# Moving the product of the next unit by one piece, in a pipelined convolution and wavelet kernel

## The chip, the cores and the metric

The kernel runs on one core of a Trainium2 chip. The metric is the device time of one execution in microseconds (us), lower is better. Engines are named as the profile names them: PE does the matrix products (PEld is its weight loads), DVE, ACT and POOL do the elementwise work, and SP issues the transfers.

## What is computed

The reference applies four layers to an image batch `x` of shape (4, 64, 256, 256): batch, channel, row, column.

```python
# layers 0, 2, 3: a long convolution in rows and columns with filters made by a small network
k = einsum('ijk,imk->ijmk', hx, hy)[0]            # separable: an x filter and a y filter per channel
y = irfft2(rfft2(x, 512) * rfft2(k, 512) / 512)[..., :256, :256]
x = y + x * bias[:, None, None]

# layer 1: mixing of channels in the Haar wavelet domain
f1 = haar2d(x)
for i in range(2):
    f3 = f1 * v[i]                                # v[i]: one value per row and column
    f4 = einsum('bchw,oc->bohw', f3, conv_w[i])   # 64 channels to 64 channels
    acc += sign(f4) * relu(abs(f4) - tau[i])      # soft threshold
x = haar2d(acc, inverse=True) + x
```

Since `v[i]` does not depend on the channel, the kernel multiplies by the channel matrix first and by `v[i]` afterwards.

## The kernel before

**Tiling.** The four images are handled as two groups of two images (`GROUPS = 2`, `NB = 2`). For the convolutions and the wavelets a round `t` holds two channels of the two images of a group, so there are 32 rounds in a group (`ROUNDS`) and 64 in all. A filter is a Toeplitz matrix. The function `toeplitz` multiplies a block of 64 rows by it with 16 small matrix products; the function `haar` applies a wavelet matrix with 4.

**Phases.** Phase A does layer 0 and the forward wavelet, round by round. Phase B does the channel mixing of layer 1, once for each group. Phase C does the inverse wavelet and layers 2 and 3, round by round. The phases are written as lists of Python functions, called pieces. The helper `beside(main, side, lead, tail)` calls the pieces of a main list in order and spreads the pieces of a side list evenly between them. The kernel sets the order of instructions by hand (`manual_schedule`): each engine executes its instructions in the order in which the pieces issue them, and semaphores make it wait where data or a buffer is not ready.

**The stretch that matters here.** The mixing of the second group, `phase_b(1)`, is the side list beside the first rounds of phase C (line 1048). The main list has 525 pieces. The side list has 404: the start with its 13 pieces, three pieces for each of 130 values of `u`, and one more. They are spread over the last 514 main pieces, which is 0.786 side pieces for each main piece: after a main piece comes one side piece or none. A step `s` of the mixing is one of 64 sets of coefficients; each step has two units, `u = 2s` and `u = 2s + 1`, one for each of the two mixings `i`. For the second group the odd units are "raw" from step 2 on (`raw`, line 573): their product is only copied out, and its threshold is done later, in phase C.

**A unit.** The product of unit `u` is `mix(u)`: four matrix products with 512 columns into the PSUM tile `f4`. This tile has one buffer:

```python
un[u]["f4"] = bps.tile([P, NB, W], F32, tag="f4", name=f"f4_{grp}_{u}", bufs=1)
```

`multiply(u)` on DVE empties it: line 670 multiplies it by `v` into `x` (even units), or line 667 copies it to `raw` (odd units). The next product can be written only when that has been done. The further steps of an even unit are `sign` (ACT, line 676), `magnitude` (ACT, line 685), `less` (DVE, line 690), `threshold` (DVE, line 695) and `add` (POOL, lines 710, 713 and 714), which accumulates into `gt`; `store` sends it to DRAM. `exchange` (ACT, line 701) swaps the two halves of an image for `add`, and `store_raw` (line 727) sends the raw product out.

The three pieces `j = 0, 1, 2` of `phase_b(1)` issue, for a value of `u`:

| piece | PE | DVE | ACT | POOL | SP |
|---|---|---|---|---|---|
| j = 0 | | `multiply(u)`, `less(u-1)` | | `add(u-2)` | `store` |
| j = 1 | `mix(u+1)` | `threshold(u-1)` | `sign(u)` | | `store_raw`, `load_v` |
| j = 2 | | | `magnitude(u)`, `exchange` | | `load_f` |

**What runs beside it.** A round of phase C has 18 pieces: 16 Toeplitz pieces (rows and columns of the layers 2 and 3; tiles `c1r`, `c1c`, `c2r`, `c2c`) and two wavelet pieces (tile `c0ps`). The results lie in PSUM banks. There are six banks for them in this stretch (`rings`, line 1044), which are used in turn, two at a time. ACT empties the row results (`ch`, line 907) and most of the wavelet results (`z`, line 895), and DVE the column results (`cy` and `o`, line 926). These copies wait in a list that is issued at the start of the following piece (`flush`). POOL does the inverse wavelet along the free axis (line 429, tiles `i` and `ci`), one operation in each main piece.

Of the kernel before, what the change touches and what calls it, by code (L numbers as in the profile page):

```python
# [67 lines left out]
GROUPS = 2  # L68
# [32 lines left out]
def conv_haar_kernel(  # L101
# [194 lines left out]
    def half(r):  # L296
        return slice(r * ROW, (r + 1) * ROW)
# [270 lines left out]
    def phase_b(grp):  # L568

        units = 2 * STEPS  # L570
        mixers = []

        def raw(u):
            return grp == GROUPS - 1 and u % 2 == 1 and FULL <= u // 2 < STEPS
# [11 lines left out]
        def load_f(s):  # L586
            if s >= STEPS:
                return
            d = st[s]
            d["f"] = bp.tile([P, NB, W], F32, tag="ft", name=f"ft_{grp}_{s}", bufs=4)  # L590
            rows, f = step_of(coef[grp], s, d["f"])
            nc.sync.dma_start(f, rows)

        def load_v(s):
            if s >= STEPS:
                return
            d = st[s]
            d["v"], d["tau"] = [], []

            def fetch(first, count, tag):  # L600
                t = bp.tile([P, 2, count, W], F32, tag=tag, name=f"{tag}_{grp}_{first}_{s}", bufs=3)
                at = slice(first * W, (first + count) * W)
                nc.sync.dma_start(t[:, 0].rearrange("p i w -> p (i w)"), v[s, :, at])
                of = thresholds[s].rearrange("r c w -> (r c) w")[:, at].unsqueeze(1).to_broadcast([2 * SHARED, C // SHARED, count * W])
                nc.sync.dma_start(t[:, 1].rearrange("p i w -> p (i w)"), of)
                d["v"] += [t[:, 0, i] for i in range(count)]
                d["tau"] += [t[:, 1, i] for i in range(count)]

            fetch(0, 2 if grp < GROUPS - 1 else 1, "v")
            if grp == GROUPS - 1 and not raw(2 * s + 1):  # L610
                fetch(1, 1, "raw")
# [20 lines left out]
        def part():  # L632

            a, b, c, d, t, u = four("g", half(0), slice(0, NB))
            op = nc.gpsimd.tensor_tensor
            op(t, a, b, ALU.add)
            op(b, a, b, ALU.subtract)
            nc.gpsimd.tensor_scalar(u, c, math.sqrt(2.0), None, ALU.mult)
            op(a, t, u, ALU.add)
            nc.gpsimd.tensor_scalar(d, d, math.sqrt(2.0), None, ALU.mult)  # L640
            op(c, b, d, ALU.add)
            op(d, b, d, ALU.subtract)
            op(b, t, u, ALU.subtract)

        def mix(u):
            s, i = divmod(u, 2)
            un[u]["f4"] = bps.tile([P, NB, W], F32, tag="f4", name=f"f4_{grp}_{u}", bufs=1)
            for b in range(NB):
                for r in range(2):
                    q = r ^ b  # L650
                    nc.tensor.matmul(  # L651
                        un[u]["f4"][half(q), b, :],
                        mixers[0][half(r), bass.ts(i, C)],
                        st[s]["f"][half(r), b],
                        start=True,
                        stop=True,
                        tile_position=(r * ROW, q * ROW),
                    )
# [5 lines left out]
        def multiply(u):  # L664
            if raw(u):
                t = st[u // 2]["raw"] = bp.tile([P, NB, W], F32, tag="raw", name=f"raw_{grp}_{u}", bufs=3)
                nc.vector.tensor_copy(t, un[u]["f4"])
                return
            un[u]["x"] = bp.tile([P, NB, W], F32, tag="x", name=f"x_{grp}_{u}", bufs=2)
            nc.vector.tensor_tensor(un[u]["x"], un[u]["f4"], both(u, "v"), ALU.mult)  # L670

        def sign(u):
            if raw(u):
                return
            un[u]["m"] = bp.tile([P, NB, W], F32, tag="m", name=f"m_{grp}_{u}", bufs=3)
            nc.scalar.activation(un[u]["m"], un[u]["x"], AF.Sign)  # L676

        def magnitude(u):
            if raw(u):
                return  # L680
            if grp == GROUPS - 1:
                un[u]["a"] = un[u]["x"]
            else:
                un[u]["a"] = bps.tile([P, NB, W], F32, tag="a", name=f"a_{grp}_{u}", bufs=1)
            nc.scalar.activation(un[u]["a"], un[u]["x"], AF.Abs)

        def less(u):
            if raw(u):
                return
            nc.vector.tensor_tensor(un[u]["a"], un[u]["a"], both(u, "tau"), ALU.subtract)  # L690

        def threshold(u):
            if raw(u):
                return
            nc.vector.scalar_tensor_tensor(un[u]["m"], un[u]["a"], 0.0, un[u]["m"], ALU.max, ALU.mult)  # L695

        def exchange(s):

            st[s]["other"] = bp.tile([P, W], F32, tag="other", name=f"other_{grp}_{s}", bufs=2)
            for q in range(2):  # L700
                nc.scalar.copy(st[s]["other"][half(q)], st[s]["f"][half(1 - q), 1])

        def add(u):
            s, i = divmod(u, 2)
            if raw(u):
                un[u].clear()
                return
            m = un[u]["m"]
            if i:
                nc.gpsimd.tensor_tensor(st[s]["g"], st[s]["g"], m, ALU.add)  # L710
            else:
                g = st[s]["g"] = bp.tile([P, NB, W], F32, tag="gt", name=f"gt_{grp}_{s}", bufs=3)
                nc.gpsimd.tensor_tensor(g[:, 0], m[:, 0], st[s]["f"][:, 0], ALU.add)  # L713
                nc.gpsimd.tensor_tensor(g[:, 1], m[:, 1], st[s]["other"], ALU.add)
            un[u].clear()

        def store(s):
            to, g = step_of(mixed[grp], s, st[s]["g"])
            nc.sync.dma_start(to, g)
            st[s].clear()  # L720

        def store_raw(s):
            if s < FULL:
                t = st[s]["raw"] = bp.tile([P, NB, W], F32, tag="raw", name=f"none_{grp}_{s}", bufs=3)
                nc.gpsimd.memset(t, 0.0)
            to, g = step_of(unshrunk, s, st[s]["raw"])
            nc.sync.dma_start(to, g)

        def piece(u, j):

            s, i = divmod(u, 2)
            if j == 0:
                if u < units:
                    multiply(u)
                if 0 < u <= units and grp == GROUPS - 1:
                    less(u - 1)
                if 1 < u <= units + 1:
                    add(u - 2)
                if i == 0 and s == 3:
                    part()  # L740
                    store(0)
                    store(1)
                if i == 0 and s > 3 and not raw(2 * s - 3):
                    store(s - 2)
                if i and raw(2 * s - 1):
                    store(s - 1)
            elif j == 1:
                if 0 < u <= units and grp < GROUPS - 1:
                    less(u - 1)
                if u + 1 < units:  # L750
                    mix(u + 1)
                if u < units:
                    sign(u)
                if i and s < STEPS and grp == GROUPS - 1:
                    store_raw(s)
                if 0 < u <= units:
                    threshold(u - 1)
                if i == 0 and s > 0:

                    load_v(s + 2)  # L760
                    if grp < GROUPS - 1:
                        load_f(s + 3)
            else:
                if i and s > 0 and grp == GROUPS - 1:
                    load_f(s + 3)
                if u < units:
                    magnitude(u)
                if i == 0 and s < STEPS:
                    exchange(s)
# [10 lines left out]
        for u in range(units + 2):  # L780
            for j in range(3):
                pieces.append(lambda u=u, j=j: piece(u, j))
        pieces.append(lambda: piece(units + 2, 0))
        return pieces

# [390 lines left out]
```

## Time and profile before

| what | value |
|---|---|
| time, median of 3 runs (lowest to highest) | 2503.36 us (2502.98 to 2511.66) |
| the profiled execution: its time and its span | 2502.12 us, 2500.3 us |
| busy PE, PEld | 91%, 74% of the span |
| busy POOL, DVE, ACT | 83%, 71%, 56% of the span |

The span runs from the first to the last instruction; the time has 1.8 us around it. "Busy" is the share of time with at least one instruction of the engine in execution. Matrix products overlap each other, so a PE that is busy is not necessarily at its full rate.

The second group's mixing (from the first product `f` to the last) lies between about 1082 and 1784 us of the span; the stretch from 1160 to 1790 us is its even part.

### The profile page before, as it was taken

To read this page: it belongs to the slowest core of one execution; us is meant where nothing else is said; L and a number is where in the kernel's file an instruction comes from. 1 tells how busy PE (TensorE), PEld (TensorE's weight loads), DVE (VectorE), ACT (ScalarE), POOL (GpSimd) and SP (SyncE) were. 2 spreads that over 40 slices of the span, in tenths; PEclk is the share of its full clock that TensorE was granted. 3 is DMA by queue.
4 is the path that set the end of the run, shared out by engine and by line. 5 is a ranking of instruction groups with operands and counts; after the bars stand their busy time and mean duration, and the time that the engine had idled before them with its cause. 6 is when DMAs were issued, how large, how long until landed. Compare 5 with 4: busy or idle time off the path is not lost.

```text
span 2500.3 us, 119287 instructions
## 1 busy us (share of the span) xinstructions
PE 2266.2 (91%) x53298; PEld 1839.1 (74%) x53298; DVE 1775.7 (71%) x1943; ACT 1392.4 (56%) x2318; POOL 2079.4 (83%) x2428
## 2 busy tenths in 40 slices
PE   7999999777777777887999999999899999999999
PEld 5777897444444444665777777777799999989998
DVE  4533335799999999765777777777577777777763
ACT  1233233577777777254666666666565655555652
POOL 2889887999999999778777877777879999999990
PEclk9999999899999999888999999999999999999999
DMA  6788888699999999557888998999866666666653
GB/s 187 249 285 293 296 304 303 253 367 357 360 339 363 342 357 330 201 203 271 314 320 315 322 327 314 323 317 326 273 208 214 208 222 217 211 209 216 216 165 111
DMA packets 222968, 688.03 MB, mean 275 GB/s; under 512 B 31470, under 2 KB 32815, under 8 KB 218232
## 3 DMA queue, kind: packets, MB, share of 16 engines
q1 hardware_dynamic: 222456, 680.40, 77.8%
q8 instruction: 419, 6.86, 1.1%
q14 instruction: 93, 0.76, 0.1%
HBM read 428.16 MB, written 252.12 MB: 272 GB/s over the span
## 4 chain that ended last, share of the span: by engine, by line
PE 45%; DVE 5%; DMA 2%; issue 2%; POOL 2%; ACT 1%; SPq 1%; DVEq 0%; ACTq 0%; POOLq 0%
PE c2c L340 10%; PE c2r L340 10%; PE c1r L340 9%; PE c1c L340 8%; PE c0ps L352 4%; PE f L651 4%; DVE m L695 1%; DVE cy L926 1%; DVE x L670 1%; DVE x L690 1%; DMA g<-mixed 1%; POOL i L429 0%; DMA rows<-in_v_rows 0%; ACT ch L907 0%; DVE o L926 0%
## 5 line engine op out<-in xcount | busy, mean ns | idle before, releaser
L429 POOL TENSOR_TENSOR i<-i,g 128x16 f32<-128x16 f32 x744 | 439.6, 612 | 27.2
L651 PE MATMUL f<-ft,mix 64*64 64x512 f32 x2048 | 290.9, 614 | 142.5 <-DVE x L670 123.0
L340 PEld LDWEIGHTS a2ps<-toep,ay 64*64 64x64 f32 x8192 | 296.0, 136 | 119.8 <-DVE f L521 48.1
L340 PE MATMUL a2ps<-toep,ay 64*64 64x128 f32 (+3 forms) x8192 | 335.4, 303 | 19.7 <-DVE f L521 15.6
L340 PEld LDWEIGHTS c2c<-toep,ch 64*64 64x64 f32 x8192 | 299.0, 135 | 58.8 <-issue 25.8
L340 PEld LDWEIGHTS c1c<-toep,ch 64*64 64x64 f32 x8192 | 299.5, 133 | 45.0 <-issue 20.3
L340 PEld LDWEIGHTS a1ps<-toep,x 64*64 64x64 f32 x8192 | 280.0, 135 | 65.1 <-issue 33.5
L429 POOL TENSOR_TENSOR ci<-i,g 128x1024 f32<-128x1024 f32 x124 | 317.5, 2581 | 4.5
L340 PE MATMUL a1ps<-toep,x 64*64 64x128 f32 (+3 forms) x8192 | 315.1, 300 | 6.1 <-DMA toep<-filt 2.4
L340 PEld LDWEIGHTS c1r<-toep,z 64*64 64x64 f32 x8192 | 294.0, 135 | 35.1 <-issue 18.0
L340 PE MATMUL c1r<-toep,z 64*64 64x192 f32 (+3 forms) x8192 | 313.5, 299 | 5.5 <-issue 3.7
L340 PE MATMUL c2c<-toep,ch 64*64 64x128 f32 (+3 forms) x8192 | 311.0, 299 | 7.7 <-ACT ch L907 7.2
L340 PEld LDWEIGHTS c2r<-toep,cy 64*64 64x64 f32 x8192 | 290.9, 134 | 29.0 <-issue 15.6
L340 PE MATMUL c2r<-toep,cy 64*64 64x192 f32 (+3 forms) x8192 | 309.9, 298 | 1.7 <-issue 1.5
L340 PE MATMUL c1c<-toep,ch 64*64 64x192 f32 (+3 forms) x8192 | 306.8, 296 | 1.7 <-ACT ch L907 1.2
L713 POOL TENSOR_TENSOR gt<-m,ft 128x512 f32<-128x512 f32 x128 | 163.6, 1278 | 159.6 <-DVE m L695 159.2
L907 ACT COPY ch<-c2r 128x512 f32<-128x512 f32 x256 | 137.3, 590 | 281.5 <-PE c2r L340 280.8
L488 ACT COPY ay<-a1ps 128x512 f32<-128x512 f32 x256 | 137.4, 589 | 273.5 <-PE a1ps L340 272.9
L676 ACT ACTIVATE m<-x 128x1024 f32<-128x1024 f32 x194 | 206.0, 1062 | 149.3 <-DVE x L670 101.0
L670 DVE TENSOR_TENSOR x<-f,v 128x1024 f32<-128x1024 f32 x192 | 233.3, 1215 | 18.5 <-PE f L651 17.9
L508 DVE SCALAR_TENSOR_TENSOR x<-x,bias_sb,a2ps 128x512 f32<-128x512 f32 x256 | 179.4, 742 | 91.4 <-POOL f L390 44.5
L926 DVE SCALAR_TENSOR_TENSOR o<-cy,bias_sb,c2c 128x512 f32<-128x512 f32 x256 | 176.8, 742 | 89.3 <-PE c2c L340 87.7
(86 smaller groups left out, 3921.5 us busy)
## 6 DMA issues: line engine op xcount, KB each, us to landing
toep<-filt SPq DMA_DIRECT2D x768, 112.0 KB
ft<-coef SPq DMA_DIRECT2D x128, 512.0 KB
mixed<-gt SPq DMA_DIRECT2D x128, 512.0 KB
g<-mixed SPq DMA_DIRECT2D x256, 256.0 KB
x<-in_x SPq DMA_DIRECT2D x128, 256.0 KB
coef<-f SPq DMA_DIRECT2D x128, 256.0 KB
x<-in_x SPq DMA_DIRECT2D x32, 1024.0 KB
v<-in_v SPq DMA_DIRECT2D x64, 512.0 KB
```

Of the source, the lines that this page charges most:

```text
L340: nc.tensor.matmul(ps[r][half(c), j % 2, k * ROW :], data[half(r), c, k, bass.ts(j, ROW)], t(r, c)[:, : N - k * ROW], start=k == 0, stop=k ...
L352: nc.tensor.matmul(ps[r][half(c)].rearrange("p h k -> p (h k)"), matrix[half(r)], pairs(r, c).rearrange("p h k -> p (h k)"), start=True, s ...
L429: engine.tensor_tensor(to, s, d, op)
L488: later(lambda y=y, ps=ps: nc.scalar.copy(y, ps))
L508: nc.vector.scalar_tensor_tensor(to, old, bias_sb[:, c : c + 1], ps, ALU.mult, ALU.add)
L651: nc.tensor.matmul(un[u]["f4"][half(q), b, :], mixers[0][half(r), bass.ts(i, C)], st[s]["f"][half(r), b], start=True, stop=True, tile_posi ...
L670: nc.vector.tensor_tensor(un[u]["x"], un[u]["f4"], both(u, "v"), ALU.mult)
L676: nc.scalar.activation(un[u]["m"], un[u]["x"], AF.Sign)
L690: nc.vector.tensor_tensor(un[u]["a"], un[u]["a"], both(u, "tau"), ALU.subtract)
L713: nc.gpsimd.tensor_tensor(g[:, 0], m[:, 0], st[s]["f"][:, 0], ALU.add)
L907: later(lambda y=y, ps=ps: nc.scalar.copy(y, ps))
L926: nc.vector.scalar_tensor_tensor(to, of, bias_sb[:, at : at + 1], ps, ALU.mult, ALU.add)
```

## The change

The call of `mix(u + 1)` is taken out of piece `j = 1` for the second group and put at the head of piece `j = 2`. For the first group it stays where it was.

```diff
             elif j == 1:
                 if 0 < u <= units and grp < GROUPS - 1:
                     less(u - 1)
-                if u + 1 < units:
+                if u + 1 < units and grp < GROUPS - 1:
                     mix(u + 1)
                 if u < units:
                     sign(u)
...
             else:
+                if u + 1 < units and grp == GROUPS - 1:
+                    mix(u + 1)
                 if i and s > 0 and grp == GROUPS - 1:
                     load_f(s + 3)
                 if u < units:
```

## The prediction

> **What bounds the kernel now.** I read the page first. POOL and PE are both above 80% over the whole span, so the page alone doesn't name a bound for the stretch that the change touches. I then asked for the busy time in two windows, both 630 us long: the even part of the second group's mixing, and the last stretch, where phase C runs with no mixing beside it.
>
> ```profile
> core 0: us, PE busy (x) PEld busy (x) DVE busy (x) ACT busy (x) POOL busy (x), PEclk, DMA share, GB/s
> 1160.00:1790.00 630.00, 597.88 (x14172) 484.51 (x14168) 459.60 (x437) 408.68 (x711) 473.83 (x520) 0.99 0.90 318
> 1850.00:2480.00 630.00, 629.54 (x17306) 594.82 (x17302) 444.36 (x504) 351.03 (x658) 557.65 (x558) 1.00 0.62 203
> ```
>
> PE is the fullest engine in both. With the mixing beside it, its weight loads are busy 77% of the time against 94% without. So PE has holes in the stretch, while DVE (73%), POOL (75%) and ACT (65%) have more. How much is lost: in the timeline two Toeplitz pieces take 2.18 us from start to start where nothing interrupts them, so one takes 1.09 us; a product `f` takes 0.86 us, and so does a wavelet piece. The stretch from 1160 us to the last product, 626.8 us, holds 200 pairs of Toeplitz pieces, 117 products and 50 wavelet pieces: 200 x 2.18 + 167 x 0.86 = 579 us. PE is therefore bound by its own work but for about 48 us.
>
> Where the 48 us are is told by the view of the tile `f` in this window, and by the list of waits.
>
> ```profile
> L651 PE MATMUL f<-ft,mix x936: 587/589/1057, 1162.2 to 1783.2; 64*64 64x512 f32 x188
> L670 DVE TENSOR_TENSOR x<-f,v x59: 1209/1217/1226, 1160.5 to 1781.4; 128x1024 f32<-128x1024 f32 x59
> L667 DVE COPY raw<-f x59: 1209/1223/1226, 1163.3 to 1783.8; 128x1024 f32<-128x1024 f32 x59
> its engine sat idle before it (us, times) until:
>   PE f L651: 48.9, 34
>   DVE x L670: 31.1, 28
> ```
>
> ```profile
> DVE o L926 <- PE c2c L340: 56.6, 29, 3.7
> DVE raw L667 <- PE f L651: 38.1, 26, 3.3
> DVE cy L926 <- PE c1c L340: 34.9, 17, 4.8
> DVE x L690 <- ACT x L685: 23.4, 22, 3.0
> PE f L651 <- DVE x L670: 21.2, 21, 2.8
> ```
>
> The row "until DVE x L670" is PE and its weight loads waiting, before a product, for DVE to empty the one buffer of `f4` (28 times). "Until PE f L651" is DVE waiting for the product. Read at the weight loads, product by product, 33 products start within 0.2 us of the end of the operation that emptied the tile, and the idle time before them sums to 32.0 us: two thirds of the 48. The longest are 2.86, 2.60, 2.17, 2.08, 1.88 and 1.84 us; about half are 0.5 to 0.65 us. One of them in the timeline (start, duration):
>
> ```profile
> 1449.18 2.71 DVE L926 SCALAR_TENSOR_TENSOR cy<-z,bias_sb,c1c 128x512 f32<-128x512 f32 x4
> 1451.81 1.21 DVE L670 TENSOR_TENSOR x<-f,v 128x1024 f32<-128x1024 f32 x1
> 1454.32 1.22 DVE L667 COPY raw<-f 128x1024 f32<-128x1024 f32 x1 [1.29 <-PE f L651]
> ...
> 1453.17 1.09 PE L651 MATMUL f<-ft,mix 64*64 64x512 f32 x8 [1.33 <-DVE x L670]
> 1454.05 1.73 PE L340 MATMUL c1r<-toep,z 64*64 64x256 f32 x40
> ```
>
> DVE is late with four residual operations, empties `f4` by 1453.02, and PE stands until then with a Toeplitz piece behind the product that needs nothing from DVE. Then DVE stands 1.29 us for the product. Each waits for the other in turn.
>
> **What the Trainium skill says.** "Perfetto Trace Analysis", section "Identifying the Most-Contended Engine", says that busy matmul time is a bad measure and the share of the weight loads a better one; the trace agrees (95% against 77% in this stretch). The same page, section "Optimization Strategy", says that the same gap repeating on the engine that should be full can mean that PSUM or SBUF lacks a buffer; `f4` with one buffer is this case. "SBUF — State Buffer", section "Who interferes with whom", says that a DVE operation with two SBUF inputs and a POOL operation that reads SBUF exclude each other. The trace agrees: `less` and `threshold` take 1541 and 1690 ns on average here, up to 3.2 us beside a `ci` of POOL, and 1228 and 1225 ns in the first group, where one input is in PSUM. That is why DVE's lateness varies.
>
> **The change, part by part.** Nothing is added or removed. In the built programs the order on DVE, ACT, POOL and SP is the same in both; only the products move on PE, each past the main pieces that lie between two side pieces. At 0.786 side pieces to a main piece this is one or two. Counted over units 10 to 127: 87 products move past one piece (0.85 or 1.07 us of PE's work), 31 past two (1.92 or 2.13); the mean is 1.32 us. Some DVE readers of `f4` and five loads of `ft` name PE among their waits in addition; the loads' waits are for products long past.
>
> Gain: `f4` is emptied at the same place of DVE's order, and PE has 0.85 to 2.13 us of other work ahead of the product. Each of the 33 waits becomes its old length less the moved work, or nothing. Summed one by one, 32.0 us become 4.9 us: the waits of about 0.6 us all go, and only some of the nine over 1.1 us leave a rest. Gain 27.1 us. At the start, from 1060 to 1160 us, products wait only 1.5 us for DVE, and PE's large wait there is 10.0 us for POOL's `ci`, which hangs on a long run of POOL; I cost that at 0.
>
> Loss one: `multiply` now follows its product by one side piece, not two. Behind it in DVE's order stand the residuals, `less`, `threshold` and the next `multiply`; ACT's `sign` and POOL's `add` wait for these, and behind `sign` stand the copies that free PSUM banks. With today's times held, a product moved by its amount, less PE's own saved wait, comes after the moment at which DVE reached it in 49 of 118 cases, by 40.5 us in all. This is idle time of DVE, not of PE. It is hidden if DVE has room: a step (two units) takes 626.8 / 58.5 = 10.7 us, DVE is busy 459.6 / 59 = 7.8 us of it, and waits 91.5 / 59 = 1.55 us for `c1c` and `c2c`, which takes up a delay of 40.5 / 59 = 0.69 us. Where it is not taken up, DVE is late at the next product and a wait of PE comes back: I put this at 3 us, with 0 and 27 us (the whole gain) as ends.
>
> Loss two: banks and POOL. Against today's reuse of a pair of banks, the copies have 1.4 to 3.0 us to spare in nine cases of ten, with a minimum of 0.25 us (`c1c`) and 0.45 us (`c2r`). A few will now be late by some tenths: 2 us, from 0 to 8. `ci` of POOL ends 1.6 to 8 us before its first product but for one case of 0.15 us; POOL waits 148.1 us for `threshold` and moves with DVE: 2 us, from 0 to 6. The queue of SP stands behind `store_raw` up to 1 us longer; the loads behind it are for two steps (21 us) or a round ahead: 0. After the stretch PE waits about 8 us, while ACT waits for the transfer of `rows`; the place in the order is the same: 0.
>
> Sum on the profiled execution: its time 2502.1 (span 2500.3 and 1.8 around it) - 27.1 + 3 + 2 + 2 = 2482.0 us. The median before is 1.2 us above that execution: 2483 us.
>
> **The rivals.** (1) The waits re-form. If DVE hangs on the product at each odd unit, its whole order shifts by as much as the product does, and `multiply` is late by the same amount at the next one: the deadline and the work move together. For it: DVE's 48.9 us of waits for the product, at least half of them in the same chain as PE's waits. Against it: the many waits of 0.6 us follow a residual, which is tied to PE and not to the last product. It leaves a gain of 0 to 12 us, say 2497 us. (2) Slower: DVE's chain becomes the bound. The place is odd `multiply`: from even `multiply` to the odd product now lie two side pieces, 2.55 main pieces or 2.7 us, and 0.96 us for the product with its signals; DVE's own 1.22 us lies inside, so DVE can be idle up to 2.4 us a step. With 7.8 us busy and 0.4 us for ACT this gives 10.6 us, even with today's step; it decides where DVE's waits for residuals do not shrink by what the product's wait grows. At 0.3 us a step more than today that is 59 x 0.3 = 18 us: 2521 us. Against it: PE ends the column pieces earlier as its own waits go. (3) No change, because the waits are the profile's artefact and the holes are of another kind (17 us of the 48 have no named releaser): 2503 us. Against it: start of the product and end of `multiply` agree to 0.15 us in 33 cases.
>
> **How the numbers follow.** Gain of 13 to 30 us: 0.65. Rival 1: 0.18. Rival 2: 0.12. Rival 3: 0.05. The forecast's own range is 2473 to 2490 us. The range for 8 in 10 reaches up through rival 1 and into rival 2: 2472 to 2512. A measurement of this kernel tells about 0.5% (12.5 us) from no change: faster 0.67, same 0.20, slower 0.13.
>
> **What would show it.** Right: the waits of `f` for DVE fall from 31 us to under 10 in the same stretch; the mixing ends some 20 us earlier; the last stretch has the same length; DVE's wait for the product stays or grows to 50 to 90 us. Wrong: PE's waits for `f` stay at 20 us or more (rival 1); PE waits for `ch`, `cy` or `o` in the stretch, or `c0ps` for `ci`, by more than 10 us; DVE's waits for `f` grow and those for `c1c` and `c2c` do not shrink (rival 2).

## The result

The changed kernel takes 2488.38 us (median of 4 runs, 2485.05 to 2488.89) against 2505.49 us before (4 runs), a ratio of 0.9932 with a 95% interval from 0.9912 to 0.9952. That is 17.1 us less; 20.4 us less had been forecast, with 2483 us. In a later set of runs the same kernel took 2485.01 us against 2503.35 us before, a ratio of 0.9917 (0.9901 to 0.9933), which is 18.3 us less. The profiled execution takes 2485.05 us, with a span of 2483.2 us (before: 2502.12 and 2500.3).

The busy time in windows, for the even part of the mixing (which now ends 13 us earlier, so the window is shorter) and for the last stretch:

```profile
core 0: us, PE busy (x) PEld busy (x) DVE busy (x) ACT busy (x) POOL busy (x), PEclk, DMA share, GB/s
1160.00:1770.00 610.00, 591.82 (x14038) 505.47 (x14030) 458.53 (x432) 405.05 (x706) 472.28 (x511) 1.00 0.92 327
1850.00:2480.00 630.00, 628.65 (x17328) 593.24 (x17320) 439.73 (x505) 343.33 (x644) 543.08 (x541) 1.00 0.61 200
```

PE's weight loads are busy 83% of the stretch, against 77% before. The last stretch is as it was (94%). The share is not a measure of pace: a kernel of the experiments below (the product two pieces later) shows 83% too, with just as many loads between 1160 and 1770 us as the kernel before has at 77% (13688 in both); it is the time with at least one load in execution, and loads overlap. The pace is therefore read from a part with fixed contents, from the start of the eleventh product to the start of the last, seen at the weight loads: 625.7 us before and 610.1 us after. PE's own work in that part (1.09 us for each of 397 Toeplitz pieces, 0.86 us for each of 117 products and 50 wavelet pieces) is 576 us in both kernels: 49 us of PE's time were lost before, and 34 us are now. The prediction, which counted 200 pairs of Toeplitz pieces, had 48 us.

From the view of the tile `f`, changed kernel, in the mixing from 1160 to 1775 us (the idle time of an engine before the operations on this tile, and how often):

```profile
its engine sat idle before it (us, times) until:
  PE f L651: 90.4, 55
  DVE x L670: 9.5, 11
```

PE's idle time before a product until DVE has emptied the tile falls from 31.1 us (28 times) to 9.5 us (11 times). DVE's idle time until the product is there rises from 48.9 to 90.4 us. Read at the weight loads, product by product, 33 waits of 32.0 us have become 10 of 6.1 us, all before the products of odd units.

The list of waits of the changed kernel in the same window, for DVE (total, times, longest):

```profile
DVE raw L667 <- PE f L651: 70.6, 37, 5.1
DVE o L928 <- PE c2c L340: 27.4, 20, 3.7
DVE cy L928 <- PE c1c L340: 22.0, 15, 2.8
DVE x L670 <- PE f L651: 19.8, 18, 2.6
```

DVE's waits for the product have grown by 41.5 us (from 48.9 to 90.4), and its waits for the column results have shrunk by 42.1 us (from 56.6 + 34.9 to 27.4 + 22.0). DVE has not more idle time than before, but waits at another place. And the list for the weight loads of the changed kernel from 1160 to 1770 us ("issue" is a wait with no named releaser):

```profile
PEld c1c L340 <- issue: 13.5, 37, 2.1
...
PEld f L651 <- DVE x L670: 6.1, 8, 1.7
PEld c1c L340 <- ACT ch L909: 4.1, 5, 2.3
PEld c2c L340 <- ACT ch L909: 3.6, 10, 0.8
```

The waits for the copies `ch` in the same window before:

```profile
PEld c1c L340 <- ACT ch L907: 2.8, 4, 2.1
...
PEld c2c L340 <- ACT ch L907: 0.3, 1, 0.3
```

Two kinds of waits have taken some of the gain. Weight loads wait for ACT's copies `ch` for 4.1 + 3.6 = 7.7 us (before: 2.8 + 0.3 = 3.1 us). And idle times of over 0.3 us before weight loads of Toeplitz pieces, with no named releaser, sum to 16.4 us in 17 holes (before: 8.5 us in 11). The expectations below counted these holes a little differently, as 15.0 us in 16 and 7.7 us in 10.

A smaller term goes the other way, and no theory below is about it. The clock that the trace shows as granted to PE (`PEclk` in the views: 0.99 before, 1.00 now) falls to half for 3.4 us twice in this part of the kernel before, never in the changed one and once in its repeat (see the end of this document). If half the work is done at half the clock, an estimate of 3.4 us was lost to it before, and of 0 and 1.7 us after.

### The profile page after: what moved, and what is told of

Its sections match the earlier page's. It is cut to its first block, busy times and chain, and to the rows that moved or that the text cites. A ratio compares the mean times of both kernels' runs of the same rounds, so it can differ in the third digit from the quotient of the medians.

```text
span 2483.2 us, 119306 instructions
## 1 busy us (share of the span) xinstructions
PE 2261.3 (91%) x53298; PEld 1863.9 (75%) x53298; DVE 1775.6 (72%) x1943; ACT 1392.2 (56%) x2318; POOL 2080.2 (84%) x2428
## 3 DMA queue, kind: packets, MB, share of 16 engines
q8 instruction: 419, 6.86, 1.1%
## 4 chain that ended last, share of the span: by engine, by line
PE 47%; DMA 2%; DVE 2%; issue 1%; POOL 1%; ACT 1%; SPq 0%; DVEq 0%; ACTq 0%; POOLq 0%
PE c2c L340 10%; PE c2r L340 10%; PE c1c L340 10%; PE c1r L340 9%; PE c0ps L352 4%; PE f L651 4%; DMA g<-mixed 1%; DMA toep<-filt 1%; DVE cy L928 0%; POOL i L429 0%; DVE x L670 0%; DMA unshrunk<-raw 0%; DVE x L690 0%; ACT ch L909 0%; DMA out<-o 0%
## 5 line engine op out<-in xcount | busy, mean ns | idle before, releaser
L651 PE MATMUL f<-ft,mix 64*64 64x512 f32 x2048 | 302.8, 614 | 117.6 <-DVE x L670 104.0
L340 PEld LDWEIGHTS c1c<-toep,ch 64*64 64x64 f32 x8192 | 311.8, 133 | 43.8 <-issue 14.0
L340 PEld LDWEIGHTS c2c<-toep,ch 64*64 64x64 f32 x8192 | 304.8, 134 | 51.1 <-issue 12.8
L340 PE MATMUL c1c<-toep,ch 64*64 64x128 f32 (+3 forms) x8192 | 317.2, 297 | 7.9 <-issue 4.6
L340 PE MATMUL a1ps<-toep,x 64*64 64x256 f32 (+3 forms) x8192 | 314.0, 299 | 6.7 <-issue 3.8
L340 PEld LDWEIGHTS c2r<-toep,cy 64*64 64x64 f32 x8192 | 298.5, 134 | 27.2 <-issue 12.5
L340 PE MATMUL c2r<-toep,cy 64*64 64x128 f32 (+3 forms) x8192 | 316.3, 298 | 2.9 <-issue 2.6
L909 ACT COPY ch<-c1r 128x512 f32<-128x512 f32 x256 | 137.5, 594 | 169.2 <-PE c1r L340 168.8
```

The costliest lines, as they stand in the source:

```text
L340: nc.tensor.matmul(ps[r][half(c), j % 2, k * ROW :], data[half(r), c, k, bass.ts(j, ROW)], t(r, c)[:, : N - k * ROW], start=k == 0, stop=k ...
L651: nc.tensor.matmul(un[u]["f4"][half(q), b, :], mixers[0][half(r), bass.ts(i, C)], st[s]["f"][half(r), b], start=True, stop=True, tile_posi ...
L909: later(lambda y=y, ps=ps: nc.scalar.copy(y, ps))
```

## The experiments

Theory A is that of the prediction: PE stood before a product until DVE had emptied the one buffer, and other work of PE now fills that time. The theories named B to E in the expectations are its rivals, or are about the two kinds of waits above.

### Odd products alone, even products alone

In the first kernel only the products of odd units move, in the second only those of even units:

```diff
-                if u + 1 < units:
+                if u + 1 < units and (grp < GROUPS - 1 or i):          # second kernel: or not i
                     mix(u + 1)
...
             else:
+                if u + 1 < units and grp == GROUPS - 1 and not i:      # second kernel: and i
+                    mix(u + 1)
```

> Only the products of the odd units are issued one piece later; the even ones stay where they were. Theory A (the time went because PE no longer stands before a product until DVE has emptied the one buffer): 31 us of PE's 32 us of waits stood before odd products. Moving these alone leaves about 11 us when the waits are shortened one by one, so the kernel should gain 12 to 18 us against before, nearly all of the change's 17; DVE's waits for the odd product (raw) rise from 38 us to about 65, those for the even product stay near 11. Rival B (DVE's chain shifts with the product, and waits come back at the next product, which is now the even one and not moved): PE's waits for DVE stay above 20 us and the gain is under 8 us.

> Only the products of the even units are issued one piece later. Theory A: few of PE's waits stand before even products, so they stay at about 26 us and the gain is 0 to 6 us. Rival B, and any theory in which the gain comes from having the product later in general: about half of the change's gain, 8 us or more. If the even move costs ACT and DVE more than it brings, the time is up to 5 us above before.

Odd alone: 2490.24 us, ratio 0.9948 (0.9935 to 0.9961), 13.1 us less than before. Even alone: 2501.34 us, ratio 0.9985 (0.9971 to 0.9998), 2.0 us less. The waits read at the weight loads:

| kernel | waits before odd products | before even products | eleventh to last product |
|---|---|---|---|
| before | 26.1 us (23) | 5.9 us (10) | 625.7 us |
| odd later | 9.5 us (10) | 3.1 us (13) | 615.3 us |
| even later | 23.0 us (25) | 0 | 624.6 us |
| both later (the change) | 6.1 us (10) | 0 | 610.1 us |

The gain is where the waits were, as theory A says, and the two parts together (15.1 us) come near to the whole. Rival B falls: when the odd products move, the waits before the unmoved even ones do not grow, they fall from 5.9 to 3.1 us. The expectation had put 31 of the 32 us before odd products; it was 26.1, read at the weight loads. With the even products alone the waits are 9 us shorter and the time only 2 us: in that profile the holes without a name are longer (13.6 us) and so, by the estimate above, is the loss at half the clock (8.5 us, in five falls).

### The product one piece earlier

```diff
             if j == 0:
                 if u < units:
                     multiply(u)
+                if u + 1 < units and grp == GROUPS - 1:
+                    mix(u + 1)
...
-                if u + 1 < units:
+                if u + 1 < units and grp < GROUPS - 1:
                     mix(u + 1)
```

> The product of the next unit is issued one piece earlier than before, right behind the operation that empties its buffer. Theory A: PE has 1.33 us less work, on average, ahead of each product, and shortens nothing: PE's waits for DVE rise from 32 us to as much as 95 us in the window of the mixing, so the kernel is slower than before by 35 to 63 us. Rival C (PE's holes at the product are not waits for the buffer, or DVE sets the pace of the stretch either way): the time stays within 10 us of before.

2563.41 us, ratio 1.0251 (1.0226 to 1.0277): 60.1 us slower. The waits before products are 82.7 us (52.2 odd, 30.5 even), 50.7 us more, and the part from the eleventh to the last product takes 685.9 us, 60.2 us more. The clock is at half nine times in this part, an estimated 15.4 us of PE's work against 3.4 us before, which covers the difference. The view of the tile `f` of this kernel, from 1160 to 1842 us:

```profile
its engine sat idle before it (us, times) until:
  issue: 100.3, 79
  DVE x L670: 49.5, 32
  PE f L651: 34.2, 23
```

Here most of PE's waiting goes by "issue"; the comparison of each product's start with the end of the operation that emptied the tile shows what it is. Rival C (DVE sets the pace either way) falls. DVE waits 15 us less for the product here than in the kernel before, and the kernel is 60 us slower.

### The product two pieces later

```diff
             if j == 0:
+                if 0 < u < units and grp == GROUPS - 1:
+                    mix(u)
                 if u < units:
                     multiply(u)
...
-                if u + 1 < units:
+                if u + 1 < units and grp < GROUPS - 1:
                     mix(u + 1)
```

> The product of a unit is issued in the same piece as the operation that empties it, one piece later than in the changed kernel. Theory A: PE's waits for the buffer are gone (under 2 us), but that is only some 5 us less than in the changed kernel; DVE's waits for the product rise to 150 us or more. If DVE has room for it, the time is 0 to 5 us below the changed kernel. If DVE's chain (7.8 us of work in a step of about 10.4 us, and now over 2 us of waits for products) becomes the bound, PE stands for ch, cy, o or ci, and the time is 5 to 40 us above the changed kernel; this I hold likelier.

2502.42 us, ratio 0.9996 (0.9983 to 1.0008): all of the gain is lost again. PE's waits for DVE are gone (0.3 us). The tile `f` and the waits of the weight loads, in this kernel:

```profile
  PE f L651: 149.4, 89
...
  DVE x L670: 0.3, 1
```

```profile
PEld c2c L340 <- ACT ch L909: 13.4, 23, 1.9
...
PEld c1c L340 <- ACT ch L909: 7.8, 13, 3.4
```

DVE waits 149.4 us for products, and PE waits 13.4 + 7.8 = 21.2 us for `ch`. The part from the eleventh to the last product takes 624.3 us, 14.2 us more than in the changed kernel. The waits for `ch` grow by 13.5 us and those before products shrink by 6; so about half of the 14 us has a named cause here, and the rest stays open. So the place of the product has a best value between two costs: early, PE waits for DVE; late, DVE's `multiply` is late, and with it ACT.

### What makes ch late

Five kernels ask why ACT is late. Its order in the third piece of an even unit is `magnitude` and the two copies of `exchange`, with `sign` in the piece before. First only the odd product goes one piece further, since no operation of ACT waits for it:

```diff
             if j == 0:
+                if i and u < units and grp == GROUPS - 1:
+                    mix(u)
...
-                if u + 1 < units and grp == GROUPS - 1:
+                if i and u + 1 < units and grp == GROUPS - 1:
                     mix(u + 1)
```

> Even products as in the changed kernel, odd ones one piece later still, in the piece of their own copy. The odd product feeds only the copy to raw, so no operation of ACT waits for it. PE's waits for DVE (6.1 us, all before odd products in the changed kernel) fall to under 1 us, DVE's wait for odd products rises from 71 to about 105 us. If PE's rest of 6 us is a plain gain: 3 to 6 us below the changed kernel. If DVE's lateness reaches PE through the even products and the residuals: equal to the changed kernel or up to 8 us above it.

2497.55 us, ratio 0.9975 (0.9962 to 0.9988), 12.5 us above the changed kernel in the same set of runs (2485.01 us). PE's waits before products fall to 2.6 us, but PE waits 18.8 us for `ch`. The reading that fits: the odd copy on DVE is late, the even `multiply` behind it is late with it (ACT waits 93.2 us for it, 76.2 in the changed kernel), and so ACT is late. The remaining 6 us of PE's waits were not to be had this way.

Next, `sign` is moved to the third piece, in the changed kernel and in the kernel with the product two pieces later:

```diff
-                if u < units:
+                if u < units and grp < GROUPS - 1:
                     sign(u)
...
+                if u < units and grp == GROUPS - 1:
+                    sign(u)
                 if u < units:
                     magnitude(u)
```

> The changed kernel with sign issued in the third piece of a unit too, just ahead of magnitude, so that ACT's copies of the second piece don't stand behind an operation that waits for multiply. If ACT's waiting for multiply (76 us) is what makes ch late for PE (7.7 us of PE's weight loads waiting for ch), the wait for multiply falls by half or more, that for ch to under 3 us, and the time by 2 to 5 us. If ch is late for another reason, both stay and the time is that of the changed kernel; it may rise by some us where less then waits longer for magnitude (6 us now).

> The product two pieces later than before, and sign in the third piece. With the product two pieces later PE had no waits for DVE, but its loads waited 21 us for ch, behind ACT's 125 us of waiting for multiply. If that blocking is what took the gain back, PE's waits for ch fall to under 8 us and the time by 8 to 14 us, to about 2490. If DVE's own chain is the bound, PE's waits for ch stay above 15 us or turn into waits for cy, o or ci, and the time stays at about 2502.

With the change: 2487.16 us, ratio 0.9928 (0.9913 to 0.9943). With the product two pieces later: 2499.39 us, ratio 0.9979 (0.9966 to 0.9993). ACT's wait for `multiply` nearly halves in both (76.2 to 40.3 us, and 125.7 to 65.9 us), but PE's wait for `ch` stays: 9.2 us, and 20.6 us. That ACT stands idle behind `sign` is therefore not the whole cause. The timeline of ACT in the changed kernel shows another. The first fence is ACT (start, duration), the second is PE's weight loads in the same microseconds:

```profile
1595.66 1.06 ACT L676 ACTIVATE m<-x 128x1024 f32<-128x1024 f32 x1 [3.93 <-DVE x L670]
1596.75 1.06 ACT L685 ACTIVATE x<-x 128x1024 f32<-128x1024 f32 x1
1597.84 1.25 ACT L701 COPY other<-ft 64x512 f32<-64x512 f32 x2
1599.11 1.56 ACT L909 COPY ch<-c1r 128x512 f32<-128x512 f32 x3
```

```profile
1598.72 0.21 PEld L352 LDWEIGHTS c0ps<-ci,inverse_sb 64*64 64x64 f32 x8
1599.74 0.20 PEld L340 LDWEIGHTS c2c<-toep,ch 64*64 64x64 f32 x4 [0.81 <-ACT ch L909]
```

When `multiply` is late, `sign`, `magnitude` and the two copies of `exchange` follow without a gap, 3.4 us in all, and only then the copies to `ch`, which free the banks for `c2c`: its weight loads stand idle for 0.81 us here. Moving `sign` leaves this row as long as it was. `exchange` does not wait for `multiply` at all. So the last two kernels issue it in the odd unit, where ACT has no `sign` and no `magnitude`:

```diff
-                if i == 0 and s < STEPS:
+                if (i if grp == GROUPS - 1 else i == 0) and s < STEPS:
                     exchange(s)
```

> The changed kernel with exchange (two copies of 0.62 us on ACT) issued in the third piece of the odd unit, where ACT has no sign and no magnitude, in place of the even one. In the changed kernel PE's longest waits for ch end after a row of sign, magnitude and two exchange copies on ACT, 3.4 us in all, with the copies to ch behind it. If that row is what makes ch late, PE's loads wait under 4 us for ch (7.7 now, 10.8 in its second profile) and the time is 2 to 6 us below the changed kernel's 2485 to 2488. If not, both stay.

> The product two pieces later than before, with exchange in the odd unit. If the row of 3.4 us behind a late multiply is what took the gain back there, PE's waits for ch fall from 21 us to under 10 and the time from 2502 by 6 to 12 us. If ch is late because multiply is late, however little stands behind it, the waits stay above 15 us and the time at about 2500.

With the product two pieces later: 2490.21 us, ratio 0.9948 (0.9927 to 0.9969), 12.2 us below the kernel without this move; against before, the two are 14.5 and 0.9 us faster. The weight loads of this kernel:

```profile
PEld c2c L340 <- ACT ch L909: 5.3, 10, 1.3
...
PEld c1r L340 <- DVE cy L928: 4.2, 9, 0.7
...
PEld c1c L340 <- ACT ch L909: 3.7, 8, 1.2
```

The wait for `ch` falls from 21.2 to 9.0 us, as expected. The row of four operations behind the late `multiply` is thus shown to have taken back most of the gain two pieces later. DVE, which waits 126.4 us for products there, does not set the pace even so: PE's weight loads wait 5.6 us for its operations `cy` (0.4 us in the changed kernel), and the part from the eleventh to the last product takes 608.1 us in the profiled execution, which is the fastest of the five.

With the change itself the move shows nothing: 2483.03 us, ratio 0.9917 (0.9889 to 0.9945), against 0.9917 for the changed kernel repeated; the wait for `ch` stays at 6.1 + 1.7 = 7.8 us, of which one wait is 4.0 us. No version here is surely faster than the changed kernel.

The traces show why. Each late copy stands at the end of a row of ACT operations that follow one another without a gap. Sorted by what the first operation of the row had waited for, PE's waits for `ch` between the eleventh and the last product are (the rest, 0.2 to 2.8 us, has other heads):

| kernel | row behind `multiply` | row behind the transfer of `g` |
|---|---|---|
| before | 0.2 us | 2.4 us |
| the change, and once more | 3.4 and 5.4 us | 3.9 and 4.8 us |
| the change, `exchange` in the odd unit | 0.5 us | 5.3 us |
| odd product two pieces later | 12.3 us | 6.3 us |
| two pieces later | 15.5 us | 5.2 us |
| two pieces later, `sign` later | 8.8 us | 9.0 us |
| two pieces later, `exchange` in the odd unit | 5.5 us | 3.3 us |

So the move of `exchange` does what was expected of it with the change too: the waits behind a late `multiply` go from 3.4 and 5.4 us to 0.5. What stays has another cause, a late transfer of `g`, the mixed images that phase C reads back from DRAM and ACT scales. In the changed kernel its longest case is this (ACT):

```profile
1166.42 0.54 ACT L406 ACTIVATE g<-g 128x16 f32<-128x16 f32 x3 [2.24 <-DMA g<-mixed]
...
1169.38 1.25 ACT L701 COPY other<-ft 64x512 f32<-64x512 f32 x2
1170.65 1.07 ACT L909 COPY ch<-c2r 128x512 f32<-128x512 f32 x2
```

The kernel before has such waits too. In the execution with `exchange` moved they are 5.3 us, and PE's waits before products are 11.5 us (6.1 and 9.8 with the change), so the time shows nothing.

### The changed kernel once more

> The changed kernel once more, on the same chip as the other three, for the comparison: 2486 to 2490 us, ratio to before 0.993 to 0.995.

2485.01 us, ratio 0.9917 (0.9901 to 0.9933). Its profile gives the spread of the smaller terms between two executions of one kernel: PE's waits before products 9.8 us (6.1 in the first), waits for `ch` 10.8 us (7.7), holes without a name 11.1 us (16.4), eleventh to last product 612.1 us (610.1).

### Fewer transfers

The holes without a name come for the most part inside a Toeplitz piece, and all but one of the weight loads that end them wait for no semaphore. In the changed kernel's trace, each of the 17 holes ends 1.3 to 1.6 us after the end of a transfer of 16384 bytes on the queue that carries instructions (such transfers follow each other at 5.6 us in the median, so chance doesn't give this). In the kernel before this holds for 8 of the 11. To see if these transfers are late among others, transfers of data were taken away, in the order of before and in the changed one:

```diff
         def load_f(s):
...
+            if grp == GROUPS - 1 and s >= 4:
+                d["f"] = kept["f", s % 4]
+                return
...
         def load_v(s):
...
+            if grp == GROUPS - 1 and s >= 3:
+                d["v"], d["tau"] = kept["v", 2]
+                return
```

> The order of before, but in the second group's mixing the loads of ft after the fourth step and of v with its thresholds after the third are left out: later steps use the tiles already loaded, so the mixed values are not the reference's; every operation of PE, DVE, ACT and POOL stays. That takes about a megabyte of some 3.4 from each step, so the DMA share in the stretch falls from 0.90 to about 0.65. PE's waits for DVE stay at 32 us (27 to 37). Holes inside Toeplitz pieces without a named releaser (7.7 us in 10 holes over 0.3 us): theory D (PE waits for the transfer of its own instructions, which is late among many data transfers) has them fall to 0 to 3 us; rival E (they have nothing to do with transfers) leaves them at 6 us or more. Time: 5 to 10 us below before by D, within 3 us of before by E.

> The same loads left out in the changed kernel. PE's waits for DVE stay near 6 us. The holes without a named releaser (15.0 us in 16 holes over 0.3 us): theory D has them fall to 0 to 4 us, and the time to 10 to 16 us below the changed kernel, so that the change brings 23 to 28 us where transfers are fewer, in place of 17. Rival E leaves them at 12 us or more, and the change brings 17 us as before.

Order of before: 2494.55 us, ratio 0.9969 (0.9954 to 0.9983). Changed order: 2476.05 us, ratio 0.9887 (0.9864 to 0.9910). The DMA share in the mixing is 0.64 and 0.66. The weight loads in the changed order with fewer loads, from 1160 to 1770 us:

```profile
PEld f L660 <- DVE x L679: 12.3, 11, 2.0
PEld c2c L340 <- issue: 9.1, 34, 0.3
...
PEld c1c L340 <- issue: 7.0, 26, 0.3
```

No hole without a name is longer than 0.3 us; with all loads they went up to 2.1 us. In the order of before, two holes of 0.9 us are left of 8.5 us. The same shows without an edit: in the last stretch of the kernel before, where the DMA share is 0.62, the holes before Toeplitz loads sum to 0.9 us in 630 us, and in the changed kernel there are none (0.5 us in its repeat). Dense transfers alone do not make them: in the first group's mixing, from 510 to 1000 us, the share is 0.97, but an instruction transfer comes only every 9 us, and the holes are 0 us before and 0.4 us in the changed kernel. So theory D is right that the holes are bound to transfers of data and of instructions. What delays these is not shown: one takes 0.96 us in the median in the changed order, with all loads and with fewer.

Theory D is wrong on what the holes did: the change brings 18.5 us here (2494.55 to 2476.05), not 23 to 28. Without the loads both orders are faster by about the same, 9 us and 9 to 12 us. And not all of that is the holes: the waits for `ch` behind a late transfer of `g` go to zero as well, and PE waits longer for DVE, 36.8 us in place of 32.0 in the order of before and 13.0 in place of 6.1 in the changed one.

## Why the prediction was right

**What bounds the stretch.** Right. PE's own work takes 576 us of it, and the time moved with PE's waits at the product: 60 us slower with 51 us more of them, 13 us faster with 19 us less (odd products alone), 2 us faster with 9 us less (even products alone).

**The gain at the buffer.** Worked out as 32.0 us to 4.9 us; measured 6.1 and 9.8 us in two executions. Product by product it came out otherwise than the sum had it. The waits of about 0.6 us are gone, but of the long ones most left no rest: where the sum had left one, 2.4 and 3.2 us were measured, not 4.9. The other 3.7 and 6.7 us stand before products where nothing was to be left (the longest that both have is 1.7 us and was 0.66 us before). These are waits that came back, for which the sum had 3 us.

**DVE's new waits are covered.** Right in mechanism and size: 40.5 us of added waits had been worked out, 41.5 us were measured, and the waits for `c1c` and `c2c` shrank by 42.1 us. This is more than two equal sums: about 37 us of the added waits stand at the products for which the working gives a delay. The forecast of 50 to 90 us of waits for the product holds at its upper end (90.4, and 95.4 us in the repeat).

**Banks and POOL.** This is the step that was off in size, in two terms. The banks were put at 2 us (0 to 8): the waits for `ch` grew from 3.1 to 7.7 and 10.8 us, by 4.6 to 7.7; the 10.8 us of the repeat even pass the 10 us that the prediction had named as a sign of being wrong. The estimate had weighed how much time the copies had to spare, but not that four operations of ACT close up behind a late `multiply` (3.2 and 5.2 us of the growth, by the table above); the rest is a later transfer of `g`. POOL was put at 2 us: `c0ps` waited for POOL at most 0.8 us in the stretch (0.3 before), so about 0.

**What the sum left out.** Of the 48 us lost, 17 had no named releaser and were taken as fixed. They contain the holes of the late transfers of instructions, 8.5 us before and 11.1 to 16.4 us after. Whether the change made them longer is not shown: over the twelve profiles with all loads they lie between 6.5 and 16.4 us, and the changed kernel with `exchange` moved has 6.7. The sum also left out the clock, which brought an estimated 1.7 to 3.4 us.

**The sum.** From the eleventh to the last product 13.6 to 15.6 us are gained, where the sum had 20, and the mixing ends 13 to 14 us earlier, where 20 had been named. The terms add up. In the first execution 25.9 us are gained before products and an estimated 3.4 by the clock, and 4.6 are lost at `ch` and 7.9 in holes: a gain of 16.8 us, where 15.6 were measured. In the second it is 22.2 and 1.7 less 7.7 and 2.6: 13.6 us, as measured. That the total came so near to the forecast is in part luck, since the terms that it did not have, holes and clock, partly cancel. The rest of the 17 to 18 us that the medians show lies outside this part. Between two profiled executions, stretches that the change does not touch differ by 2 to 4 us too: the first product comes 2.8 us later in the changed kernel's, and from the start of the last product to the end it takes 713.3 us, where the kernel before takes 717.7 and the repeat 714.4.

**The rivals.** None came true as a whole. Waits that re-form (rival 1) took 3.7 to 6.7 us, not the gain; that they move to the next product is refuted by the odd move alone. DVE's chain as the bound (rival 2) did not appear even with the product two pieces later, once `exchange` was out of the way, but for the 5.6 us of waits for `cy`; there ACT was in the way first, which the rival had not named. That the waits are not real (rival 3) is refuted by the kernel with the product one piece earlier.

## What to carry to other kernels

Where an engine waits at a single buffer and has other work behind that instruction, look at where the buffer is emptied and where it is refilled in the two orders, and give each side about the time that it is short of; here a second piece gave back all that the first had brought. Before a product is put later, look at what stands in order behind its reader, on the reader's engine and on the next one: operations that close up behind a late one make the copies late that free PE's banks. When an added wait is to be called free, show which other wait of that engine shrinks by it.

## What the runs showed of the hardware

The transfers of PE's own instructions can stop PE. The page counts 419 transfers of instructions on one queue, 6.86 MB, so 16384 bytes each. PE and PEld together executed 106596 instructions, and PE's sequencer (semaphores and the like) 691 more, which makes 256 for one transfer; so it is taken that this queue carries PE's. The Trainium skill, "Runtime: NRT & Kernel Launch", section "Instruction fetch mechanics", says that instructions are refilled in blocks of this size by a transfer of the engine's own and that the cost is mostly hidden. The trace agrees on the size. It was hidden at a DMA share of 0.66 (no hole over 0.3 us), and not at 0.90 to 0.92, where holes of up to 2.1 us summed to 8.5 and 16.4 us in 610 us. At that share, taking a megabyte of data from each step gave 9 to 12 us of time without touching an instruction on PE; part of this is ACT, which no longer waited for the transfer of `g`.

PE's idle time can cost twice, as a fall of the clock follows it. In the fourteen profiles the granted clock falls to half 24 times between the eleventh and the last product, mostly for 3.4 us. In the 3.4 us ahead of each fall PE had started 0 to 32 weight loads, where Toeplitz pieces without a hole have about 100 (32 in 1.09 us); none of over 32 was followed by a fall, and in the stretches of this length without a fall behind them there were at least 20. The kernel with the product one piece earlier, in which PE waits most, has nine falls, the kernel before two, the changed kernel none.
